# A 5x5 convolution by seven products per column instead of eight, for the first of four images

## The chip, the cores and the metric

The kernel runs on one core of a Trainium2 chip. The metric is the device time of one execution, in microseconds (us); the median of three executions is given.

## What is computed

The input x is four images of 128 channels and 64 x 64 pixels, in fp32. Four layers follow each other, each on the normalised x (a group norm over groups of four channels), each added to x:

```
x = x + attention(gn(x))            # all 4096 pixels of an image against each other
x = x + conv2d(gn(x), c, 5x5, pad 2)  # c built from two tables of weights by radius
x = x + scan(gn(x))                 # two directions, 64 channels and 64 states each
x = x + conv2d(gn(x), main_w, 3x3, pad 1) + main_b
```

The change concerns the second layer. Written for two neighbouring rows of the output, with r0 to r5 the six padded input rows under them and w0 to w4 the five rows of taps (each a row of five matrices of 128 x 128, one for each column dx), it is

```
y0 = w0 r0 + w1 r1 + w2 r2 + w3 r3 + w4 r4
y1 = w0 r1 + w1 r2 + w2 r3 + w3 r4 + w4 r5
```

which is ten products per column for a pair of rows.

## The kernel before

**The order of the images.** Channels lie on the 128 partitions, pixels along the free dimension. `program` writes the whole order out by hand, as generators: `front` makes attention, the 5x5 convolution and the operands of the scan for one image, and `scan_core` the scan. The front of image b+1 runs beside the scan of image b, piece by piece, by a budget of PE time per step. Image 0 has no scan before it, so its front runs alone: first a loop steps it until `(0, "attended")` is ready, later `before(0)` steps it until the scan's operands of image 0 are there. While image 0 is in attention, two setup generators are woven in, four steps of the front for one of theirs: `scan_constants` and `build_conv_weights`, which fills `cw` (25 matrices, and two sums of rows of taps, `SUM12` = w1 + w2 and `SUM34` = w3 + w4). In this time a pool `fill` holds side sums of the softmax (`side_sums`, on VectorE and GpSimd in turn; for the other images PE sums). The pool `tables` holds what the weights are built from.

**The convolution** is `conv_pairs`. It normalises the image in four quarters on ScalarE (`piece`, L369) into a padded image `xpe` with rows of 66 elements. GpSimd makes differences of neighbouring rows (`odd` L684, `even` L692) into `df`. The output is done in four chunks of 16 rows: eight even and eight odd ones. For each chunk three banks are accumulated, each from groups of five matmuls (L760), one for each column dx:

```
q   = (w1+w2) r2 + (w3+w4) r4
pe0 = w0 r0 + w1 (r1-r2) + w3 (r3-r4)      y0 = q + pe0
pe1 = w0 r1 + w2 (r3-r2) + w4 (r5-r4)      y1 = q + pe1
```

These are eight products for ten. A bank is taken out while the next one is filled: the closure `done` of a bank is called after the third matmul of the next. For the first image `q` is copied by ScalarE and added to both rows of `xs` by GpSimd (L775); for the others (`lean`) an identity matmul adds it on PE. `add` (L736) adds pe0 and pe1 to `xs` on VectorE with sums for the next norm, and ScalarE squares them (L313).

**After it** `scan_prep` and `scan_operands` normalise again, make the scan's operands and store them; `scan_core` loads them back (`br`, `cr`, `de`, `dx`) and GpSimd multiplies (`db`, L1027), VectorE scans (L1037), GpSimd or VectorE multiplies (L1058, L1040), PE sums over the states (L1072).

A program with a second path for softmax sums out of range follows; it isn't taken.

Of the kernel before, what the change touches and what calls it, by code (L numbers as in the profile page):

```python
# [24 lines left out]
F32 = mybir.dt.float32  # L25
I32 = mybir.dt.int32
AF = mybir.ActivationFunctionType
ALU = mybir.AluOpType
# [4 lines left out]
P = 128  # L33
# [5 lines left out]
PAD = 2  # L39
# [6 lines left out]
PRODUCT, HOP, SLOT, PACE, ENDPACE, AHEAD = 0.86, 1.7, 0.7, 2.8, 1.5, 4  # L46
# [6 lines left out]
def conv_preact_kernel(  # L53
# [16 lines left out]
    nc = tc.nc  # L70
    B, C, H, W = x.shape
# [17 lines left out]
    dram = ctx.enter_context(tc.tile_pool(name="dram", bufs=2, space=DRAM))  # L89
    ps = ctx.enter_context(tc.tile_pool(name="ps", bufs=1, space=PSUM))  # L90
    pools, ready = {}, set()

    def bank(tag, name):
        return pools.get(tag, ps).tile([P, MM], F32, tag=tag, name=name)
# [40 lines left out]
    for d in range(2):  # L135
        r = slice(d * HALF, (d + 1) * HALF)
# [81 lines left out]

    SUM12, SUM34 = 5, 6
    cw = const.tile([P, NTAP + 10, C], F32, name="cw")
    taps5 = cw[:, :NTAP, :]

# [59 lines left out]
    def large(n, name):  # L284
        return pools["big"].tile([P, ASIZE], F32, tag=f"A{n % 2}", name=name)
# [82 lines left out]
    def normalise(dst, src, gn):  # L368
        nc.scalar.activation(dst, src, AF.Identity, scale=gn[0], bias=gn[1])  # L369
# [292 lines left out]

    def conv_pairs(b, xs, tag, st, st2, lean):

        NP, CK = H // 2, CH // W // 2
        WQ = W + PAD
        xp = large(b, f"xpe_{b}")
        rows = xp[:, : HP * WQ].rearrange("p (h w) -> p h w", w=WQ)  # L670
        xh = xs.rearrange("p (h w) -> p h w", w=W)
        nc.gpsimd.memset(rows[:, :PAD, :], 0.0)
        nc.gpsimd.memset(xp[:, (HP - PAD) * WQ : HP * WQ + PAD], 0.0)
        nc.gpsimd.memset(rows[:, PAD : HP - PAD, :PAD], 0.0)
        gn = yield from group_norm(st, f"e{b}")
        diffs = pools["big"].tile([P, VSIZE], F32, tag="V", name=f"df_{b}")
        nc.gpsimd.memset(diffs[:, 2 * (NP + 1) * WQ :], 0.0)

        def piece(i):
            h0, h1 = i * H // 4, (i + 1) * H // 4  # L680
            normalise(rows[:, PAD + h0 : PAD + h1, PAD:], xh[:, h0:h1, :], gn)

        def odd(j, n):
            nc.gpsimd.tensor_tensor(  # L684
                diffs[:, j * WQ : (j + n) * WQ].rearrange("p (h w) -> p h w", w=WQ),
                rows[:, 2 * j + 1 : 2 * (j + n) : 2, :], rows[:, 2 * j + 2 : 2 * (j + n) + 1 : 2, :],
                ALU.subtract,
            )

        def even(j, n):  # L690
            at = (NP + j) * WQ
            nc.gpsimd.tensor_tensor(  # L692
                diffs[:, at : at + n * WQ].rearrange("p (h w) -> p h w", w=WQ),
                rows[:, 2 * j + 1 : 2 * (j + n) : 2, :], rows[:, 2 * j : 2 * (j + n) - 1 : 2, :],
                ALU.subtract,
            )

        def differences(i):
            last = i == 3
            odd(8 * i, 8 + last)  # L700
            even(8 * i + 1, 8 + last)

        def by_rows(t, n):

            return [t[:, o : o + n * WQ].rearrange("p (h w) -> p h w", w=WQ) for o in (0, PAD)]

        padded, differ = by_rows(xp, HP), by_rows(diffs, 2 * (NP + 1))

        def image(r, dx):
            late = dx // PAD > 0  # L710
            dx -= late * PAD
            return padded[late][:, r : r + 2 * CK - 1 : 2, dx : dx + W]

        def diff(r, dx):
            late = dx // PAD > 0
            dx -= late * PAD
            return differ[late][:, r : r + CK, dx : dx + W]

        def chunk(t, c, y):

            v = t[:, bass.ts(c, CH)].rearrange("p (h t w) -> p h t w", t=2, w=W)
            return v[:, :, y, :]

        def flat(t):
            return t.rearrange("p (h w) -> p h w", w=W)

        piece(0)
        yield HOP / 2
        piece(1)
        differences(0)  # L730
        K5 = 5
        steps, done = [], None

        def add(c, y, acc):
            i = 2 * c + y
            nc.vector.scalar_tensor_tensor(  # L736
                chunk(xs, c, y), flat(acc), 1.0, chunk(xs, c, y), ALU.mult, ALU.add,
                accum_out=st2.sum(i),
            )
            st2.squares(i, chunk(xs, c, y), xs[:, 0:1])  # L740

        for c in range(L // CH):
            j = c * CK
            if c < 2:
                piece(2 + c)
            if c < 3:
                differences(c + 1)
            accs = [
                (bank("s", f"pq_{b}_{c}"), ((SUM12, image, 2 * j + 2), (SUM34, image, 2 * j + 4))),
                (bank("a", f"pe0_{b}_{c}"),  # L750
                 ((0, image, 2 * j), (1, diff, j), (3, diff, j + 1))),
                (bank("z", f"pe1_{b}_{c}"),
                 ((0, image, 2 * j + 1), (2, diff, NP + j + 1), (4, diff, NP + j + 2))),
            ]
            for n, (acc, parts) in enumerate(accs):
                k, total = 0, len(parts) * K5
                for w, view, r in parts:
                    for dx in range(K5):
                        k += 1
                        nc.tensor.matmul(  # L760
                            flat(acc), cw[:, w * K5 + dx, :], view(r, dx),
                            start=k == 1, stop=k == total and (n == 0 or not lean),
                        )
                        if k == 3 and done is not None:
                            done()
                            done = None
                        if k % 3 == 0:
                            yield 3 * PRODUCT
                if n == 0:
                    qs = pools["bg"].tile([P, MM], F32, tag="w", bufs=4, name=f"q_{b}_{c}")  # L770

                    def done(acc=acc, qs=qs, c=c):
                        nc.scalar.copy(qs, acc)
                        for y in range(0 if lean else 2):
                            nc.gpsimd.tensor_tensor(  # L775
                                chunk(xs, c, y), chunk(xs, c, y), flat(qs), ALU.add
                            )
                    yield PRODUCT
                else:
                    if lean:  # L780
                        nc.tensor.matmul(acc, ident, qs, start=False, stop=True)
                        yield PRODUCT

                    def done(acc=acc, c=c, y=n - 1):
                        add(c, y, acc)
        yield HOP
        done()

# [351 lines left out]


    def program(safe):
        mats4, ynds, ends = {}, {}, {}
        ready.clear()
        if safe:
# [94 lines left out]
        inner, last = range(PER, NM - PER), range(NM - PER, NM)  # L1242
# [15 lines left out]
        with ExitStack() as es, tc.manual_schedule():  # L1258
# [19 lines left out]
            if not safe:  # L1278
                with tc.tile_pool(name="fill", bufs=2) as pools["fill"]:
                    while not (0, "begun") in ready:  # L1280
                        next(work)

                    with tc.tile_pool(name="tables", bufs=1) as tmp:
                        for _ in chain(scan_constants(), build_conv_weights(tmp)):
                            for _ in range(4):
                                next(work)
                    while (0, "attended") not in ready:
                        next(work)
                del pools["fill"]
                setup.close()  # L1290
# [32 lines left out]
            for _ in chain(end(B - 1, range(PER)), back(B - 1)):  # L1323
                pass

    program(False)
    lower.close()

# [12 lines left out]
    with tc.If(again > 0):  # L1341
        program(True)
# [59 lines left out]
```

## Time and profile before

| what | value |
|---|---|
| time, median of 3 | 4534.42 us (4531.9 to 4534.6) |
| span of the profiled execution | 4538.3 us |
| mean granted TensorE clock | 0.939 |
| PE busy | 4022.5 us, 89% |
| DVE busy | 3649.1 us, 80% |
| POOL busy | 3636.2 us, 80% |
| ACT busy | 2400.1 us, 53% |
| DMA | 719.48 MB, 159 GB/s on average |

The busy times are of the whole span, but the stages differ. Attention of image 0 lasts until about 507 us, its convolution from there to 653 us, and the scan's first multiplication is at 705 us. From then to about 3520 us the scan of one image runs beside the front of the next; after that the last scan runs beside the last layer of the first three images.

In the profile PE is TensorE's matmuls, PEld its loads of weights, DVE VectorE, ACT ScalarE, POOL GpSimd. A matmul of 512 columns in fp32 leaves two records.

### The profile page before, as it was taken

The page shows a single profiled execution, that of the slowest core. Times are in us where ns is not written, and L with a number is a line of the kernel's source. Part 1 is how long each engine was busy: PE and PEld are TensorE (multiplying, and loading weights), DVE is VectorE, ACT ScalarE, POOL GpSimd, SP SyncE. Part 2 cuts the span into 40 slices and gives each one's busy share as a digit, 9 for nine tenths or more (in the row PEclk, how much of TensorE's full clock was granted, in tenths as well). Part 3 has the DMA queues.
Part 4 walks back from the last instruction along what each step waited for, and adds up shares of the span by engine and source line. Part 5 has one row for each costly group of instructions (what it writes and reads, how often), then busy time and mean ns, then how long its engine had stood idle before and what let it go on. Part 6 is the DMA issues. An engine that isn't in the chain of part 4 may idle for free. (4 is left out here: it accounts for less than half of the span.)

```text
span 4538.3 us, 43660 instructions
## 1 busy us (share of the span) xinstructions
PE 4022.5 (89%) x13568; PEld 1492.3 (33%) x13568; DVE 3649.1 (80%) x3619; ACT 2400.1 (53%) x4420; POOL 3636.2 (80%) x1730
## 2 busy tenths in 40 slices
PE   8999998999999979999999879999999658576767
PEld 4444433333333323333333223333333112121212
DVE  4722106999998978999989879999999699999993
ACT  3333217666665466666654566666654654544441
POOL 3433207999998969999989889999999799999992
PEclk9999999999999989999999989999999878687878
DMA  1000006445544555544545555545445566656561
GB/s 62 6 1 1 5 29 239 175 170 174 175 174 155 181 202 201 175 174 169 179 154 181 185 207 180 169 170 175 175 159 178 211 235 204 231 188 230 186 232 47
DMA packets 210579, 719.48 MB, mean 159 GB/s; under 512 B 24864, under 2 KB 25760, under 8 KB 210208
## 3 DMA queue, kind: packets, MB, share of 16 engines
q1 hardware_dynamic: 208736, 715.87, 44.8%
q8 instruction: 109, 1.79, 0.2%
q14 instruction: 134, 1.10, 0.1%
q10 hardware_dynamic: 1600, 0.73, 0.1%
HBM read 649.07 MB, written 67.44 MB: 158 GB/s over the span
## 5 line engine op out<-in xcount | busy, mean ns | idle before, releaser
L1027 POOL TENSOR_TENSOR db<-dx,br 128x1024 f32<-128x1024 f32 x1024 | 2399.7, 2366 | 234.0 <-DMA dx<-dxd 59.7
L1020 ACT ACTIVATE da<-de,a_neg 128x512 f32<-128x512 f32 (+1 forms) x1795 | 1342.2, 751 | 745.4 <-DVE da L1037 451.2
L464 PE MATMUL sc<-r,x 128*128 128x512 f32 x2048 | 1082.4, 611 | 18.2 <-ACT r L433 12.4
L476 PE MATMUL acc<-pt,v 128*128 128x512 f32 x2048 | 1046.6, 593 | 1.6
L1058 POOL TENSOR_TENSOR hc<-hc,cr 128x1024 f32<-128x1024 f32 x406 | 959.7, 2364 | 14.3 <-ACT last L1053 11.7
L470 ACT ACTIVATE pt<-sc 128x512 f32<-128x512 f32 x1024 | 604.3, 590 | 563.9 <-PE sc L464 555.2
L1072 PE MATMUL y<-hc,sel 128*32 128x512 f32 x4096 | 656.9, 651 | 271.5 <-POOL hc L1058 267.0
L1040 DVE TENSOR_TENSOR hc<-da,cr 128x512 f32<-128x512 f32 (+1 forms) x1067 | 828.4, 776 | 68.9 <-issue 1.8
L1037 DVE TENSOR_TENSOR_SCAN da<-da,last,db 128x512 f32<-128x512 f32 (+1 forms) x464 | 728.2, 1569 | 27.3 <-POOL db L1027 21.7
L1037 DVE TENSOR_TENSOR_SCAN da<-da,da,db 128x512 f32<-128x512 f32 x449 | 577.9, 1287 | 13.6 <-ACT da L1020 12.7
L464 PEld LDWEIGHTS sc<-r,x 128*128 128x128 f32 x2048 | 359.1, 190 | 605.0 <-issue 374.3
L476 PEld LDWEIGHTS acc<-pt,v 128*128 128x128 f32 x2048 | 387.5, 190 | 497.2 <-issue 477.9
L1037 DVE TENSOR_TENSOR_SCAN hc<-da,hc,db 128x512 f32<-128x512 f32 x322 | 413.1, 1283 | 61.2 <-ACT da L1020 30.4
L1037 DVE TENSOR_TENSOR_SCAN hc<-da,last,db 128x512 f32<-128x512 f32 (+1 forms) x304 | 455.9, 1500 | 6.6 <-ACT da L1020 2.4
L518 POOL TENSOR_TENSOR sidep<-sidep,pt 128x512 f32<-128x512 f32 x120 | 170.4, 1420 | 280.0 <-ACT pt L470 277.9
L1072 PEld LDWEIGHTS y<-hc,sel 128*32 128x32 f32 x4096 | 94.7, 111 | 728.5 <-POOL hc L1058 359.5
L643 PE MATMUL pcm<-xpm,cw 128*128 128x512 f32 x576 | 290.5, 652 | 30.5 <-ACT xpm L369 30.5
L760 PE MATMUL pe<-df,cw 128*128 128x512 f32 x640 | 289.5, 598 | 0.0
L518 DVE TENSOR_TENSOR sided<-sided,pt 128x512 f32<-128x512 f32 x120 | 97.2, 810 | 231.0 <-ACT pt L470 229.7
L1037 DVE TENSOR_TENSOR_SCAN da<-da,db 128x512 f32<-128x512 f32 (+1 forms) x154 | 231.2, 1501 | 32.5 <-POOL db L1027 16.4
L498 PE MATMUL zp<-pt,ones 128*32 128x512 f32 x1536 | 204.8, 595 | 5.0 <-DVE xs L562 5.0
L1053 ACT COPY last<-da 128x1 f32<-128x1 f32 x469 | 73.0, 156 | 246.9 <-DVE hc L1040 245.1
(196 smaller groups left out, 2719.5 us busy)
## 6 DMA issues: line engine op xcount, KB each, us to landing
br<-bm SPq DMA_DIRECT2D x512, 512.0 KB, 5.2
cr<-cm SPq DMA_DIRECT2D x512, 512.0 KB, 3.9
de<-dd SPq DMA_DIRECT2D x64, 512.0 KB, 4.6
dx<-dxd SPq DMA_DIRECT2D x64, 512.0 KB, 6.5
x<-in_x_dram SPq DMA_DIRECT2D x16, 512.0 KB, 5.1
xs<-in_x_dram SPq DMA_DIRECT2D x16, 512.0 KB, 5.6
xsd<-xs SPq DMA_DIRECT2D x16, 512.0 KB, 5.1
xcd<-xc SPq DMA_DIRECT2D x16, 512.0 KB, 2.8
```

Of the source, the lines that this page charges most:

```text
L464: nc.tensor.matmul(sc, xn[:, bass.ts(j, P)], rq[blk], start=True, stop=True)
L470: nc.scalar.activation(pt, sc, AF.Exp)
L476: nc.tensor.matmul(acc[blk], v[:, j, :], ring[:, u % NRING, :], start=j == 0, stop=j == NJT - 1)
L518: eng.tensor_tensor(s, s, ring[:, u % NRING, :], ALU.add)
L643: nc.tensor.matmul(acc.rearrange("p (r w) -> p r w", w=W), weights[:, t, :], xp[:, y : y + RPM, dx : dx + W], start=t == 0, stop=t == k * ...
L760: nc.tensor.matmul(flat(acc), cw[:, w * K5 + dx, :], view(r, dx), start=k == 1, stop=k == total and (n == 0 or not lean),)
L1020: nc.scalar.activation(da, rep["de", b, c, d, g][:, bass.ts(h, size)], AF.Exp, scale=a_neg[:, at(i)])
L1027: nc.gpsimd.tensor_tensor(dbs[i], rep["dx", b, c, d, g], rows["b", b, c, d, q], ALU.mult)
L1037: nc.vector.tensor_tensor_scan(h, da, db[:, cut], before, ALU.mult, ALU.add)
L1040: nc.vector.tensor_tensor(hc[:, cut], h, rows["c", b, c, d, q][:, cut], ALU.mult)
L1058: nc.gpsimd.tensor_tensor(hcs[i], hcs[i], rows["c", b, c, d, q], ALU.mult)
L1072: nc.tensor.matmul(y[r : r + SG, :], sel, hcs[i - KG + 1 + gg][:, bass.ts(h, MM)], start=q == 0, stop=False, tile_position=(0, r), skip_gr ...
```

## The change

For the first image the three upper rows of taps are done in another way. With three sums of rows, t = r1 + r2, f = r0 - r2 and l = r3 - r1, and two more rows of matrices, HSUM = (w0 + w1 + w2) / 2 and HDIF = (w0 - w1 + w2) / 2:

```
q   = (w3+w4) r4 + HSUM t
pm  = HDIF (r1-r2)
pe0 = w0 f + w3 (r3-r4)                    y0 = q - pm + pe0
pe1 = w2 l + w4 (r5-r4)                    y1 = q + pm + pe1
```

These are seven products for ten. The sums of rows are made by VectorE (`combine`, three instructions for each quarter, into `combos`), the matrices by VectorE too (`more_weights`, four instructions, woven in behind `build_conv_weights`). pm has a bank of its own (tag `y`) and is taken out by VectorE, subtracted from the even rows and added to the odd ones. `combos` and `more` lie in the pool `fill`, which therefore stays open until the convolution is done. The other three images are left as they were.

The diff, cut to its core:

```diff
+    def more_weights(to):
+        w = [cw[:, n * 5 : (n + 1) * 5, :] for n in range(3)]
+        half, dif = to[:, 0], to[:, 1]
+        nc.vector.tensor_tensor(half, w[0], w[2], ALU.add)
+        yield HOP
+        nc.vector.tensor_scalar(half, half, 0.5, None, ALU.mult)
+        yield HOP
+        nc.vector.scalar_tensor_tensor(dif, w[1], -0.5, half, ALU.mult, ALU.add)
+        yield HOP
+        nc.vector.scalar_tensor_tensor(half, w[1], 0.5, half, ALU.mult, ALU.add)
+        yield HOP
...
+        wide = pools.get("fill") if not lean else None
+        if wide:
+            NC = NP * WQ + PAD
+            combos = wide.tile([P, 3, NC], F32, tag="combos", bufs=1, name="combos")
+            nc.gpsimd.memset(combos[:, :, NP * WQ :], 0.0)
+            views = [by_rows(combos[:, n, :], NP) for n in range(3)]
+
+        def combine(j, n):
+            for m, (p, q, op) in enumerate(
+                ((1, 2, ALU.add), (0, 2, ALU.subtract), (3, 1, ALU.subtract))
+            ):
+                a, b_ = (rows[:, 2 * j + r : 2 * (j + n) + r - 1 : 2, :] for r in (p, q))
+                nc.vector.tensor_tensor(views[m][0][:, j : j + n, :], a, b_, op)
+
         def differences(i):
             last = i == 3
+            if wide:
+                combine(8 * i, 8)
             odd(8 * i, 8 + last)
             even(8 * i + 1, 8 + last)
...
+            if wide:
+                total, first, last = (combo(n) for n in range(3))
+                accs = [
+                    (accs[0][0], (accs[0][1][1], (HSUM, total, j))),
+                    (bank("y", f"pm_{b}_{c}"), ((HDIF, diff, j),)),
+                    (accs[1][0], ((0, first, j), (3, diff, j + 1))),
+                    (accs[2][0], ((2, last, j), (4, diff, NP + j + 2))),
+                ]
...
+                elif wide and n == 1:
+                    def done(acc=acc, c=c):
+                        for y, op in enumerate((ALU.subtract, ALU.add)):
+                            nc.vector.tensor_tensor(
+                                chunk(xs, c, y), chunk(xs, c, y), flat(acc), op
+                            )
...
+                    more = pools["fill"].tile([P, 2, 5, C], F32, tag="more", bufs=1, name="more")
 
                     with tc.tile_pool(name="tables", bufs=1) as tmp:
-                        for _ in chain(scan_constants(), build_conv_weights(tmp)):
+                        for _ in chain(scan_constants(), build_conv_weights(tmp), more_weights(more)):
                             for _ in range(4):
                                 next(work)
-                    while (0, "attended") not in ready:
+                    while (0, "convolved") not in ready:
                         next(work)
                 del pools["fill"]
                 setup.close()
```

More of the change, by code (lines that the diff above doesn't have):

```diff
@@ L91, in conv_preact_kernel @@
     pools, ready = {}, set()
+    more = None
     def bank(tag, name):
@@ L217, in scan_constants @@
         yield HOP
-    SUM12, SUM34 = 5, 6
+    SUM12, SUM34, HSUM, HDIF = 5, 6, 7, 8
     cw = const.tile([P, NTAP + 10, C], F32, name="cw")
@@ L677, in conv_pairs, with by_rows @@
         nc.gpsimd.memset(diffs[:, 2 * (NP + 1) * WQ :], 0.0)
+        def by_rows(t, n):
+            return [t[:, o : o + n * WQ].rearrange("p (h w) -> p h w", w=WQ) for o in (0, PAD)]
         def piece(i):
@@ L696, in even @@
             )
+        wide = pools.get("fill") if not lean else None
[10 more added lines that the diff above has]
+                nc.vector.tensor_tensor(views[m][0][:, j : j + n, :], a, b_, op)
         def differences(i):
             last = i == 3
+            if wide:
+                combine(8 * i, 8)
             odd(8 * i, 8 + last)
             even(8 * i + 1, 8 + last)
-        def by_rows(t, n):
-            return [t[:, o : o + n * WQ].rearrange("p (h w) -> p h w", w=WQ) for o in (0, PAD)]
         padded, differ = by_rows(xp, HP), by_rows(diffs, 2 * (NP + 1))
@@ L717, in diff, with combo, view @@
             return differ[late][:, r : r + CK, dx : dx + W]
+        def combo(n):
+            def view(r, dx):
+                late = dx // PAD > 0
+                dx -= late * PAD
+                return views[n][late][:, r : r + CK, dx : dx + W]
+            return view
         def chunk(t, c, y):
@@ L760, in conv_pairs @@
                         nc.tensor.matmul(
-                            flat(acc), cw[:, w * K5 + dx, :], view(r, dx),
-                            start=k == 1, stop=k == total and (n == 0 or not lean),
+                            flat(acc), cw[:, w * K5 + dx, :] if w < HSUM else more[:, w - HSUM, dx, :],
+                            view(r, dx), start=k == 1, stop=k == total and (n == 0 or not lean),
                         )
@@ L782, in conv_pairs, with done @@
                         yield PRODUCT
-                    def done(acc=acc, c=c, y=n - 1):
+                    def done(acc=acc, c=c, y=n - len(accs) + 2):
                         add(c, y, acc)
@@ L787, in conv_pairs @@
         done()
+        ready.add((b, "convolved"))
     def scan_prep(b, xs, st, mats4):
@@ L1144, in program @@
     def program(safe):
+        nonlocal more
         mats4, ynds, ends = {}, {}, {}
```

## The prediction

> **What bounds the kernel now.** I read the page first (busy shares, slices), then the table of busy time by stretch, then the first image's convolution in the waits and the timeline.
>
> From the page, the slices (113 us each; columns are tenths busy):
>
> ```profile
> span 4538.3 us, 43660 instructions
> PE   8999998999999979999999879999999658576767
> DVE  4722106999998978999989879999999699999993
> POOL 3433207999998969999989889999999799999992
> ```
>
> In slices 2 to 5 only PE is full. From slice 6 on, VectorE and GpSimd (the scan) are full as well. The changed convolution lies in slices 4 and 5, where nothing runs beside it. The stretches (columns: us, then busy PE, PEld, DVE, ACT, POOL, granted clock, DMA share, GB/s):
>
> ```profile
> 513.30:653.40 140.10, 140.02 (x320) 61.01 (x320) 4.89 (x14) 11.61 (x22) 18.80 (x16) 0.99 0.01 4
> 653.40:697.00 43.60, 33.76 (x118) 11.57 (x120) 12.03 (x28) 27.69 (x43) 5.73 (x7) 0.92 0.45 168
> 780.00:1500.00 720.00, 702.87 (x2626) 259.40 (x2630) 673.96 (x706) 441.17 (x886) 666.89 (x296) 0.99 0.49 170
> ```
>
> The convolution takes 140.1 us and PE is busy in 140.0 of them; DVE works 4.9 us and POOL 18.8. What PE waits for between 514 and 652 us is a single line, the wait that ends as the stage begins:
>
> ```profile
> PE pq L760 <- ACT xpe L369: 7.6, 1, 7.6
> ```
>
> So the stage is bound by the number of matmuls. The timeline gives their price and the stage's two ends (start, duration, what, and in brackets the idle time before it):
>
> ```profile
> 512.01 3.51 ACT L369 ACTIVATE xpe<-xs,nb_e,rs_e 128x1024 f32<-128x1024 f32 x3 [3.91 <-POOL df L677]
> 513.30 10.78 PE L760 MATMUL pq<-xpe,cw 128*128 128x512 f32 x20 [7.65 <-ACT xpe L369]
> ...
> 523.92 4.49 PE L760 MATMUL pe<-xpe,cw 128*128 128x512 f32 x10
> 528.24 8.75 PE L760 MATMUL pe<-df,cw 128*128 128x512 f32 x20
> ...
> 558.39 1.89 PE L760 MATMUL pe<-xpe,cw 128*128 128x512 f32 x4
> ...
> 653.43 0.69 DVE L736 SCALAR_TENSOR_TENSOR xs<-pe,xs 128x512 f32<-128x512 f32 x1 [12.22 <-PE pe L760]
> ```
>
> A matmul leaves two records: 320 records, 4 chunks of 40 matmuls. From 523.92 to 558.39 runs exactly one chunk: 34.47 us / 40 = 0.862 us each. The first ten took 10.62 us instead of 8.62: about 2.0 us go to the slow clock at the start. PE starts at 513.30, as the first of three normalising pieces ends; at the far end VectorE's last addition is released by PE at 653.43.
>
> Behind it everything hangs on that end. GpSimd's queue:
>
> ```profile
> 689.46 2.49 POOL L889 TENSOR_TENSOR delta<-delta,u 128x512 f32<-128x512 f32 x2 [30.55 <-ACT u L913]
> ...
> 705.14 2.35 POOL L1027 TENSOR_TENSOR db<-dx,br 128x1024 f32<-128x1024 f32 x1 [10.75 <-DMA br<-bm]
> ```
>
> GpSimd waits 30.55 us for this image's operands, and the scan's first product waits for a transfer of rows just written by this image. No clock, other image or earlier load sets the start of the scan.
>
> [...] PE idles 7.65 us, then loses about 2.0 us in its first ten matmuls. The idle gap only grows, so this loss stays. [...] The trace has 692 ns (the scan's multiply, L1040, 780 to 3500 us) and 1825 ns for 1600 elements. [...] between 100 and 230 us, where both sum, the side sums take 1053 ns on DVE and 1760 on POOL, against 0.69 and 1.27 us apart.
>
> **The change, part by part.**
>
> *Removed and replaced on PE.* Each chunk had 8 groups of five matmuls (2 in pq, 3 in each pe); now 7 (2 in pq, 1 in pm, 2 in each pe). Four chunks: 160 becomes 140. Same shape, both operands fp32, views of the same stride for diffs and combos (rows back to back, as diffs had). 20 x 0.862 = 17.2 us off a stage in which PE never waits.
>
> *The start.* Before, the first five matmuls read the rows of the first normalised quarter alone; now the first group is SUM34, whose rows begin two lower and reach into the second quarter. The three pieces take 3.51 us together, 1.17 each: PE starts at about 514.47 instead of 513.30. Cost 1.2 us, on the path.
>
> *Three sums of rows, 12 on VectorE.* 12 x 0.71 = 8.5 us, in a stage where DVE works 4.9 of 140. PE waits for them at two kinds of place. First chunk: the fourth matmul of the second group reads two elements over the edge and so needs the fourth sum. Six sums and four differences are queued on DVE and POOL from 513.3 on; [...] they take 6 x 0.71 + 4 x 1.12 (POOL L684, L692) = 8.7 us and end at 522.0. PE asks at 514.47 + 2.0 + 8 x 0.862 = 523.4. Hidden, by a margin of 1.4 us. Later chunks: the sums wait for the normalised piece, which ACT does behind the squares of pe0; from pe0's end that is 0.3 + 0.8 (DVE) + 1.1 + 1.2 (ACT) + 0.7 = 4.1 us, and PE has 18 matmuls, 15.5 us, before it asks. Hidden behind pe1. What queues behind a waiting sum on DVE is the addition of pe1, which no one needs within a chunk.
>
> *pm's eviction, 8 on VectorE.* One PSUM and one SBUF input, nearest row L561, 0.69 us: 5.5 us. Each pair waits for POOL's additions of q (2 x 1.27), released about 0.8 us after pq ends; pm's own five matmuls take 4.3. A bank of its own (y), unused until the scan. Hidden.
>
> *The two matrices.* Four instructions of 640 elements during attention. Bounds: [...] 1.29 by the nearest row, L274 (beside POOL); together 3.3 to 5.2 us. I take the high end. There DVE lags behind the side sums by up to 5.7 us (a sum ready at 182.0 runs at 187.7), with the added one 7.0. The ring has 8 places of 1.72 us, 13.7 us, so ScalarE doesn't wait for a place and PE doesn't either. Cost 0.
>
> *Moved.* The early pools close after the convolution instead of after attention. The scan's tiles keep their places and their first loads come later anyway. On every engine the order outside these instructions is unchanged. Cost 0.
>
> *Sum.* -17.2 + 1.2 = -16.0 us; the last addition at about 637.4 instead of 653.43, and all behind it earlier by the same. 4534.4 - 16.0 = 4518.4 us.
>
> **The rivals.**
>
> R1, part of the gain is lost on the spot. For: the margin of 1.4 us at the first chunk, DVE's lag in the build of the weights[...]. Against: PE's single wait in the stage. Two of the three together cost about 2 to 6 us: 4520 to 4524, say 4523.
>
> R2, the gain doesn't reach the end. The scan stage (POOL 93% busy from 780 to 1500 us) would have to start when it did before, because another wait takes over: 4534. For: PE, DVE and POOL are all near full later, so a different phase of transfers could cost some us. Against: the 30.55 us wait above; nothing on POOL or DVE between 653 and 689 us comes from elsewhere.
>
> R3, slower: PE waits for the new sums in every chunk. If each chunk began with its three sums, two differences and two additions in series (2.1 + 2.2 + 2.5 = 6.9 us) and PE stood still meanwhile, 27.6 us would be lost: 4518.4 + 27.6 = 4546. Against: the operations are issued a chunk ahead, as the differences are now, and PE waits for none of those.
>
> R4, more than the count: later stages fall into a better phase, 4510. Nothing speaks for it.
>
> **How the numbers follow.** Forecast 0.77, R1 0.13, R2 0.05, R3 0.03, R4 0.02. The predicted time is the forecast's, 4518.4. The range takes in R1 and the scatter of the three times (4531.9 to 4534.6) with some us for phases of the scan on both sides: 4512 to 4525.5. Within 0.2% means over 4525.4. Faster: forecast, R1, R4, 0.92; same: R2, 0.05; slower: R3, 0.03.
>
> **What would show it.** Right: 280 records of matmuls in the stage, beginning about 514.5 and ending near 637; no PE wait in it; four groups of DVE sums near 0.7 us; a first db near 689. Start wrong: PE begins at 513.3. R1: a wait of PE for combos, or for pt in attention. R2: POOL's first db still near 705. R3: four waits on DVE inside the stage. The forecast fails if the first db moves by 16 us and the end doesn't.

## The result, and the profile after

The changed kernel takes 4521.68 us (median of 10 executions, 4515.17 to 4524.64), the kernel before 4534.45 us beside it (10 executions, 4529.49 to 4536.89). The ratio is 0.9971, with a 95% interval of 0.9963 to 0.998: 12.8 us shorter, between 9.1 and 16.8. The forecast was 4518.4 us, with a range of 4512 to 4525.5.

The page of the changed kernel, the lines for its span and the busy slices (113 us each):

```profile
span 4517.3 us, 43608 instructions
...
PE   8999998999999979999999879999999658575767
DVE  4721217999998978999989879999999799999992
POOL 3433308999998969999989789999999899999992
```

The slices are counted from 0. VectorE's slices 4 and 5 went from 1 and 0 tenths to 2 and 1: that is the new work, in a stage where it was nearly idle. In slice 6 VectorE went from 6 to 7 and GpSimd from 7 to 8: the scan begins earlier in that slice.

Busy time by stretch of the changed kernel (us, then busy PE, PEld, DVE, ACT, POOL, clock, DMA share, GB/s):

```profile
513.00:636.50 123.50, 121.94 (x280) 53.30 (x280) 21.51 (x35) 11.63 (x22) 20.87 (x18) 0.98 0.01 5
636.50:681.00 44.50, 34.97 (x122) 11.79 (x122) 12.39 (x29) 28.18 (x43) 5.59 (x5) 0.92 0.47 171
```

280 records instead of 320: 20 matmuls fewer. PE is busy for 121.94 us, where it was 140.02. VectorE works 21.51 us instead of 4.89. What PE waits for between 512 and 636 us is still one line:

```profile
PE pq L808 <- ACT xpe L370: 8.9, 1, 8.9
```

No sum, no eviction and no difference holds PE up. The wait in front of the first matmul grew from 7.6 to 8.9 us. The timeline shows the two ends and the first chunk (start, duration, what, in brackets the idle time before it), first what feeds PE, then PE, then the way to the scan:

```profile
511.74 3.51 ACT L370 ACTIVATE xpe<-xs,nb_e,rs_e 128x1024 f32<-128x1024 f32 x3 [3.90 <-POOL nb_e L365]
...
513.01 7.48 DVE L731 TENSOR_TENSOR combos<-xpe 128x528 f32<-128x528 f32 x6 [2.21 <-ACT xpe L370]
...
513.06 1.62 POOL L705 TENSOR_TENSOR df<-xpe 128x528 f32<-128x528 f32 x1 [1.28 <-ACT xpe L370]
...
514.25 5.95 PE L808 MATMUL pq<-xpe,cw 128*128 128x512 f32 x10 [8.87 <-ACT xpe L370]
520.04 4.46 PE L808 MATMUL pq<-combos,more 128*128 128x512 f32 x10
524.33 4.46 PE L808 MATMUL pm<-df,more 128*128 128x512 f32 x10
528.62 4.46 PE L808 MATMUL pe<-combos,cw 128*128 128x512 f32 x10
...
545.79 4.49 PE L808 MATMUL pq<-xpe,cw 128*128 128x512 f32 x10
...
575.87 4.49 PE L808 MATMUL pq<-xpe,cw 128*128 128x512 f32 x10
...
636.23 0.69 DVE L776 SCALAR_TENSOR_TENSOR xs<-pe,xs 128x512 f32<-128x512 f32 x1 [7.89 <-PE pe L808]
...
672.30 2.49 POOL L944 TENSOR_TENSOR delta<-delta,u 128x512 f32<-128x512 f32 x2 [30.59 <-ACT u L968]
...
687.28 2.37 POOL L1082 TENSOR_TENSOR db<-dx,br 128x1024 f32<-128x1024 f32 x1 [10.07 <-DMA br<-bm]
```

PE starts 514.25 - 511.74 = 2.51 us behind the first normalising instruction; before it was 513.30 - 512.01 = 1.29. The groups that read sums or differences take 4.29 us for five matmuls. One chunk, from 545.79 to 575.87, takes 30.08 us where it took 34.47. The stage, from its first normalising instruction to its last addition, is 124.49 us long where it was 141.42: 16.9 us less. The scan's first db comes 17.9 us earlier than in the profile of before (705.14). Both are one pair of profiles; further ones follow below.

### The profile page after: what moved, and what is told of

It reads as the page before. It is cut to its first block, busy times and chain, and to the rows that moved or that the text cites. A ratio compares the mean times of both kernels' runs of the same rounds, so it can differ in the third digit from the quotient of the medians.

```text
span 4517.3 us, 43608 instructions
## 1 busy us (share of the span) xinstructions
PE 3996.2 (88%) x13528; PEld 1482.2 (33%) x13528; DVE 3667.9 (81%) x3643; ACT 2399.5 (53%) x4420; POOL 3638.5 (81%) x1731
## 5 line engine op out<-in xcount | busy, mean ns | idle before, releaser
L1113 POOL TENSOR_TENSOR hc<-hc,cr 128x1024 f32<-128x1024 f32 x406 | 960.1, 2365 | 17.6 <-ACT last L1108 15.1
L1092 DVE TENSOR_TENSOR_SCAN da<-da,last,db 128x512 f32<-128x512 f32 (+1 forms) x464 | 728.1, 1569 | 24.1 <-POOL db L1082 17.6
L1092 DVE TENSOR_TENSOR_SCAN da<-da,da,db 128x512 f32<-128x512 f32 x449 | 577.9, 1287 | 14.3 <-ACT da L1075 13.4
L808 PE MATMUL pe<-df,cw 128*128 128x512 f32 x560 | 255.2, 598 | 0.0
```

The lines of the kernel that those rows point to most:

```text
L808: nc.tensor.matmul(flat(acc), cw[:, w * K5 + dx, :] if w < HSUM else more[:, w - HSUM, dx, :], view(r, dx), start=k == 1, stop=k == total ...
L1092: nc.vector.tensor_tensor_scan(h, da, db[:, cut], before, ALU.mult, ALU.add)
L1113: nc.gpsimd.tensor_tensor(hcs[i], hcs[i], rows["c", b, c, d, q], ALU.mult)
```

## The experiments

All times are compared with executions of the kernel before on the same chip. A difference in us is that of the two medians. The ratio with its interval weighs all executions, so it needn't be the ratio of the medians; where only five executions were made the two can lie 2 to 4 us apart. The kernels with matmuls left out no longer compute the convolution; they only price the matmuls. "Matmuls" are those of the first image's convolution unless others are named.

**The changed kernel again, and matmuls left out of the kernel before.** The time had fallen by 12.8 us, the stage in the profile by 16.9. Either a part is lost behind the stage, or the additions cost something, or single executions scatter too much for the difference to mean anything. The first four kernels ask this.

The changed kernel, unaltered:

> The changed kernel unaltered, as the yardstick for the runs on the same chip. Theory S (every us taken off the first convolution reaches the end, the missing 3 us of the first comparison are scatter between executions): 16 to 18 us faster than the kernel before. Theory L (a fixed few us, or a quarter, are lost in the later stages): 12 to 13.5 us faster again.

Measured: 4518.57 us against 4532.9; 14.3 us shorter, ratio 0.9969 (0.9958 to 0.998). It lies between the two theories and doesn't choose. Its profile shows one source of scatter. The first two groups of PE:

```profile
516.09 7.53 PE L808 MATMUL pq<-xpe,cw 128*128 128x512 f32 x10 [8.87 <-ACT xpe L370]
523.46 4.46 PE L808 MATMUL pq<-combos,more 128*128 128x512 f32 x10
```

The first five matmuls took 7.37 us here and 5.79 in the profile above, behind the same idle time of 8.87 us; five at a granted clock of 1.00 take 4.29. The slow start costs 3.1 us in one execution and 1.5 in the other.

Twenty matmuls left out of the kernel before:

```diff
+            if not lean:
+                accs[2] = (accs[2][0], accs[2][1][:2])
```

> The kernel before without its last group of five matmuls in pe1 of the first image (w4 times r5-r4 is left out of the odd rows): 20 matmuls fewer, none of the new sums, no later start. Theory S: first db 17.2 us earlier and the time 17.2 us shorter. Theory L: db 17.2 us earlier and the time 13 us shorter. Theory V (what the change adds on VectorE or the pool held longer costs the 3 us): 17.2 us here, and only some 13 in the changed kernel on the same chip.

Measured: 4512.48 us against 4532.9; 20.4 us shorter, ratio 0.9959 (0.9945 to 0.9972), which is 18.6 us (12.7 to 24.9). Its first db is at 689.13 us, 176 us behind the first normalising instruction where it was 193. No loss shows on the way to the end; theory L's 13 us lies at the interval's edge.

Forty left out:

```diff
+            if not lean:
+                accs[1:] = [(t, parts[:2]) for t, parts in accs[1:]]
```

> As the run with 20 matmuls fewer, and the last group of pe0 left out too (w3 times r3-r4 of the even rows, w4 times r5-r4 of the odd ones): 40 matmuls fewer. Theory S: 34.5 us shorter. Theory L with a fixed loss of 4 us: 30.5. Theory L with a quarter lost: 26.

Measured: 4497.07 us; 35.8 us shorter, ratio 0.9929 (0.9916 to 0.9943), which is 32 us (25.8 to 38.1). The medians say theory S, the ratio lies between theory S and a fixed loss of 4 us. A loss of a quarter stands at the very edge of the interval; a fixed loss can't be excluded by this run alone.

Sixty left out of the other three images, where the scan runs beside the convolution:

```diff
+            if lean:
+                accs[2] = (accs[2][0], accs[2][1][:2])
```

> The kernel before with the last group of pe1 left out for the other three images (w4 times r5-r4 of their odd rows), 60 matmuls fewer where the scan runs beside them. If PE sets the pace there as in the first image: 51.7 us shorter. If GpSimd and VectorE set it: within 5 us of the kernel before. I expect the second, 0 to 10 us shorter.

Measured: 4528.81 us against 4532.9; 4.1 us shorter, ratio 0.9994 (0.9986 to 1.0003). 51.7 us of PE's work are gone and about a tenth of it shows at most (6.3 us at the interval's edge). The stretch from 1500 to 2500 us of this kernel:

```profile
1500.00:2500.00 1000.00, 949.20 (x3450) 350.53 (x3448) 918.23 (x980) 602.12 (x1157) 907.22 (x410) 0.98 0.52 181
```

PE is 95% busy there, as in the kernel before, yet its matmuls aren't what is paid for. VectorE and GpSimd are at 92 and 91%; that they set the pace there agrees with this, but isn't shown by it. The first image is the place for this change, since there a matmul taken away shows in the time.

**The start and the clock.** Two kernels price the two terms at the stage's beginning, a third has both edits. The quarters of normalising cut one row later:

```diff
             h0, h1 = i * H // 4, (i + 1) * H // 4
+            if not lean:
+                h0, h1 = h0 + (i > 0), min(h1 + 1, H)
```

> The changed kernel with the first image's quarters of normalising cut one row later (17, 16, 16 and 15 rows), so that the first group of matmuls needs only the first piece. If the later start costs what I priced: PE begins 1.3 us after the first normalising instruction instead of 2.5, and the time is 1.1 us shorter than the changed kernel's (some 15 us shorter than the kernel before), which the trace shows and the times hardly can. If the first group waits for something else as well: no change in PE's beginning.

Measured: 4518.26 us against 4532.9; 14.6 us shorter, ratio 0.9967 (0.9955 to 0.9979). ScalarE and PE at the start:

```profile
510.89 3.56 ACT L370 ACTIVATE xpe<-xs,nb_e,rs_e 128x1088 f32<-128x1088 f32 x3 [3.90 <-POOL nb_e L365]
...
512.24 6.21 PE L810 MATMUL pq<-xpe,cw 128*128 128x512 f32 x10 [7.70 <-ACT xpe L370]
```

PE follows after 1.35 us instead of 2.51. The later start was the wait for the second piece and nothing else. In the time it doesn't stand out, as expected.

Eight matmuls without use in PE's idle time:

```diff
+        if not lean:
+            idle = bank("y", f"idle_{b}")
+            for _ in range(8):
+                nc.tensor.matmul(
+                    idle, ident, cw[:, :4, :].rearrange("p k c -> p (k c)"), start=True, stop=True
+                )
         gn = yield from group_norm(st, f"e{b}")
```

> The changed kernel with eight matmuls of 512 columns, whose result nothing reads, put into PE's idle time in front of the first convolution. If the slow clock after that idle time costs 1.5 to 3 us and differs from execution to execution: the ten matmuls of the first bank take 8.6 us instead of 10 to 12, and the time is 1.5 to 3 us shorter than the changed kernel's. If the clock is no part of the missing time: the same as the changed kernel.

Measured: 4520.56 us; 12.3 us shorter, ratio 0.9972 (0.9961 to 0.9983): no gain over the changed kernel. The timeline and the clock (third number from the end of each line in the second fence, PE's busy time behind the comma) say why:

```profile
505.31 7.03 PE L695 MATMUL idle<-cw,ident 128*128 128x512 f32 x16
514.34 6.25 PE L814 MATMUL pq<-xpe,cw 128*128 128x512 f32 x10 [2.00 <-ACT xpe L370]
520.42 4.46 PE L814 MATMUL pq<-combos,more 128*128 128x512 f32 x10
```

```profile
510.96:514.37 3.41, 1.42 (x5) 0.38 (x3) 1.28 (x2) 2.55 (x3) 2.05 (x5) 1.00 0.00 0
514.37:517.78 3.41, 3.41 (x4) 1.42 (x5) 3.41 (x3) 0.95 (x1) 3.41 (x3) 0.50 0.00 0
517.79:519.79 2.00, 2.00 (x6) 0.94 (x5) 2.00 (x2) 0.00 (x0) 1.59 (x2) 1.00 0.00 0
```

The eight ended 2.00 us too soon. Just as the convolution began, at 514.37, the clock went to half, and the first five matmuls took 6.08 us. The expectation failed: the filling left 2.00 us of idle time in front of the stage, and the start stayed slow.

Both edits:

> Both edits together: the stage from the first normalising instruction to the last addition takes 1.3 + 140 x 0.86 + 0.4 = 122 us instead of 124.5 to 126; 2.6 to 4 us shorter than the changed kernel, 17 to 19 us shorter than the kernel before.

Measured: 4514.07 us against 4532.9; 18.8 us shorter, ratio 0.9956 (0.9943 to 0.997). PE and the clock again:

```profile
506.01 7.03 PE L695 MATMUL idle<-cw,ident 128*128 128x512 f32 x16
513.88 4.59 PE L816 MATMUL pq<-xpe,cw 128*128 128x512 f32 x10 [0.83 <-ACT xpe L370]
518.31 4.46 PE L816 MATMUL pq<-combos,more 128*128 128x512 f32 x10
```

```profile
513.00:515.00 2.00, 1.17 (x4) 0.65 (x4) 1.14 (x2) 2.00 (x3) 1.09 (x1) 1.00 0.00 0
515.00:517.00 2.00, 2.00 (x6) 0.79 (x5) 2.00 (x2) 1.10 (x1) 2.00 (x2) 1.00 0.00 0
```

With the earlier start the gap is 0.83 us, the clock stays at 1.00, and the first five matmuls take 4.43 us. The last addition of the stage comes 121.97 us after its first normalising instruction, as expected, and 2.5 us sooner than in the changed kernel's profile. By its median this is the fastest kernel that leaves nothing out, but its interval overlaps with the changed kernel's.

**What the additions cost.** Each sum of rows issued twice:

```diff
-                nc.vector.tensor_tensor(views[m][0][:, j : j + n, :], a, b_, op)
+                for _ in range(2):
+                    nc.vector.tensor_tensor(views[m][0][:, j : j + n, :], a, b_, op)
```

> The changed kernel with each of the twelve sums of rows issued twice: 8.5 us more on VectorE. If the sums are hidden, as priced: the time of the changed kernel, within its scatter, except at the first chunk, where twelve sums and four differences in series end at about 526 us and PE asks for the fourth sum at 523.4: up to 3 us there. If the sums cost the missing 3 us: another 3 us or more in every chunk's waits, and a time 3 to 8 us longer.

Measured: 4518.32 us, 14.6 us shorter than before, ratio 0.9968 (0.9956 to 0.9979): what the changed kernel gives. The sums of the first two quarters and all of PE's waits in the stage:

```profile
513.79 11.68 DVE L732 TENSOR_TENSOR combos<-xpe 128x528 f32<-128x528 f32 x12 [2.21 <-ACT xpe L370]
```

```profile
PE pq L809 <- ACT xpe L370: 8.9, 1, 8.9
```

Twice the sums still hide, at the first chunk too. The twelve end at 525.47, as expected, but PE needs only the first four: the fourth is written for the second time by 522.75, and PE asks for it at 523.7. The 3 us allowed for the first chunk didn't come.

After these eight the kernels with the new products came out some 2 us short of what their stage gains, and those with matmuls left out did not. The last four ask about that. The changed kernel with its additions, but the old eight groups on PE, in two runs:

```diff
-            if wide:
+            if False:
                 total, first, last = (combo(n) for n in range(3))
...
-                elif wide and n == 1:
+                elif False:
```

> The changed kernel with all its additions but the old eight groups of matmuls: the sums of rows and the two matrices are made on VectorE and the pool is held, nothing reads them. So far the kernels with the new products come out some 2 us short of what their stage gains, the two with matmuls left out do not (both with intervals of 2 to 3 us). Theory V, the additions cost it: 2 to 3 us slower than the kernel before. Theory S, scatter: the same as the kernel before within 1.5 us.

> The same kernel once more, for more executions: the same expectations.

Measured: 4533.9 and 4533.71 us against 4533.32, 13 executions of this kernel each; both ratios 1.0001 (0.9992 to 1.0009). The medians are 0.6 and 0.4 us longer, and the intervals exclude a cost of more than some 4 us for the sums, the matrices and the pool held longer. Theory V's 2 to 3 us lie inside these intervals; the 26 executions taken together average 0.2 us more than the 26 of the kernel before, which speaks against it. pm's eviction is not in this kernel. The changed kernel's profile has it, here in the last chunk:

```profile
619.13 1.28 DVE L830 TENSOR_TENSOR xs<-xs,pm 128x512 f32<-128x512 f32 x2 [12.28 <-PE pm L808]
...
627.64 0.69 DVE L776 SCALAR_TENSOR_TENSOR xs<-pe,xs 128x512 f32<-128x512 f32 x1 [7.23 <-PE pe L808]
```

VectorE has taken pm out 7.23 us before PE releases the next addition, so this eviction holds nothing up in the stage.

> The changed kernel once more, beside the one with 20 matmuls left out on the same chip. Theory S: 1 to 2 us slower than that one (its later start of 1.2 us), 16 us faster than before. Theory V or L: 3 to 5 us slower than that one, 13 to 14 us faster than before.

> The kernel with 20 matmuls left out (w4 times r5-r4 of the first image's odd rows) once more: 17.2 us faster than before by theory S, 13 to 14 by theory L.

Measured: the changed kernel 4517.99 us, 15.3 us shorter, ratio 0.9967 (0.9955 to 0.9979); with 20 matmuls left out 4514.41 us, 18.9 us shorter, ratio 0.9963 (0.9949 to 0.9977). The medians differ by 3.6 us, within the 3 to 5 of theories V and L; the ratios lie 1.8 us apart, within the 1 to 2 of theory S. With 6 and 5 executions that is no choice.

**Where the executions scatter.** The time from the first db to the end of the span, from each profile (span minus start of db):

| kernel | first db, us | span, us | from db to the end, us |
|---|---|---|---|
| before | 705.14 | 4538.3 | 3833.2 |
| additions only, two runs | 706.37, 705.72 | 4529.3, 4531.6 | 3822.9, 3825.9 |
| 20 matmuls left out, two runs | 689.13, 687.39 | 4514.7, 4510.0 | 3825.6, 3822.6 |
| 40 matmuls left out | 672.06 | 4490.6 | 3818.5 |
| changed, three runs | 687.28, 691.93, 687.91 | 4517.3, 4519.1, 4514.3 | 3830.0, 3827.2, 3826.4 |
| changed, each sum twice | 689.07 | 4513.9 | 3824.8 |
| changed, start cut; PE filled; both | 686.37, 688.16, 687.26 | 4515.7, 4517.8, 4517.7 | 3829.3, 3829.6, 3830.4 |

Within one kernel the rest of the program varies by several us between profiles. The value of the kernel before stands apart: its profile is of an execution of 4540.09 us, longer than any of the 69 timed executions of this kernel (4526.5 to 4537.8). With it, the six profiles with the old products average 3824.8 us from the first db to the end, without it 3823.1. The seven with the new products average 3828.3. So the profiles don't show that all of the stage's gain reaches the end. They rather speak for 3 to 5 us more behind the first db in the kernels with the new products, but single differences of this size are no more than the scatter.

## Why the prediction was right

**The price of a matmul.** Forecast 20 x 0.862 = 17.2 us. PE's waits inside the stage are none, and four chunks, each 34.47 - 30.08 = 4.39 us shorter, give 17.6 us. The 0.4 us more come from the mix: five matmuls take 4.29 us in the groups that read sums or differences and 4.32 or 4.33 in those that read the padded image (523.92 to 528.24 before, 545.79 to 550.12 after), and six of the seven groups are now of the first kind, four of the eight before. Shown, by the profile and by the kernels with 20 and 40 matmuls left out.

**The later start.** Forecast 1.2 us; the profile has 2.51 - 1.29 = 1.22, and cutting the quarters one row later takes it back. Shown.

**The slow clock.** I took its 2.0 us for a constant, an estimate from one trace. The start of the changed kernel lost 1.5 and 3.1 us in two executions. The stretches at half rate, in the kernel before, the changed kernel and its repeat:

```profile
506.89:517.12 10.23, 3.81 (x5) 1.75 (x6) 2.89 (x15) 4.32 (x5) 4.57 (x7) 0.50 0.00 0
506.84:517.07 10.23, 2.81 (x4) 1.29 (x5) 6.72 (x19) 4.32 (x5) 4.83 (x7) 0.50 0.00 0
505.07:522.12 17.05, 8.08 (x15) 4.30 (x16) 11.25 (x22) 4.32 (x5) 7.06 (x8) 0.50 0.00 0
```

Half rate ended 3.8, 2.8 and 6.0 us after PE's first matmul (513.30, 514.25 and 516.09), and half of that is about what each lost. In the traces of the kernel before and the changed kernel the granted clock is either 1.00 or 0.50, and every stretch between two changes is a multiple of 3.413 us; the stretches above are three, three and five times that long. The moment of the change shifts against PE's work: half rate began 1.2 and 1.5 us after PE's idle time had begun in the first two, and 2.2 us before it in the repeat. For the mean the constant is fair (five profiles with the new products and no filling lose 2.0 us on average), for a single execution it isn't. With it the stage's gain in the first pair of profiles comes out: 17.6 - 1.2 + 0.5 = 16.9 us.

**The sums.** Forecast hidden, by 1.4 us at the first chunk, with the six sums and four differences one after the other, which was an estimate. Its 0.71 us for a sum lies on the line through two lengths that the kernel before shows (692 ns for 512 elements, 1825 ns for 1600), which gives 709 ns for 528. Six sums at the 0.70 us of the later ones would take 4.2 us; they took 7.48, the slowest of them 1.63, and a difference 1.62 us where it was 1.10. They ended at 520.49. PE asked at 520.04 + 3 x 0.86 = 522.6: a margin of 2.1 us. The two engines do slow each other here, but less than by whole instructions one after the other, which would be the 8.7 us of the forecast. The later sums took 0.70 us each, as forecast. Issued twice the sums are hidden still.

**pm's eviction.** Forecast 8 x 0.69 us on VectorE, hidden. The median of the eight is 0.684 us, and VectorE is done with it 7 us before its next work. Shown, by the profile.

**The matrices.** Forecast 3.3 to 5.2 us on VectorE, hidden; the lower bound was an estimate, 0.82 us for each of the four (the same line gives 825 ns for 640 elements). The tile's instructions in the changed kernel (min/median/max in ns, and the start):

```profile
L673 DVE TENSOR_TENSOR more<-cw x1: 1883/1883/1883, 187.4 to 187.4; 128x640 f32<-128x640 f32 x1
L675 DVE TENSOR_SCALAR more<-more x1: 1558/1558/1558, 190.6 to 190.6; 128x640 f32<-128x640 f32 x1
L677 DVE SCALAR_TENSOR_TENSOR more<-cw,more x1: 819/819/819, 193.5 to 193.5; 128x640 f32<-128x640 f32 x1
L679 DVE SCALAR_TENSOR_TENSOR more<-cw,more x1: 820/820/820, 199.5 to 199.5; 128x640 f32<-128x640 f32 x1
```

Together 5.1 us; two of the four are stretched to twice the others. The convolution's first normalising instruction is at 511.74 instead of 512.01. In all the profiles it lies between 510.9 and 513.6, and the changed kernel's three (511.7 to 513.6) are among those of the kernels with the old products (511.7 to 513.3), so no loss in attention shows.

**The way to the end.** Forecast: all behind the stage is earlier by the same, 16.0 us. Stage and first db did that: between the kernels with the old products and nothing left out and the changed kernel, in the mean of three profiles each, the stage is 16.6 us shorter and the first db 16.7 us earlier. The times say 12.8, 14.3 and 15.3 us in three comparisons. 16.0 lies within each interval, but each median falls short of it. The means of the same executions differ by 13.1, 14.1 and 15.1 us, 14.1 on average; by the scatter of the executions I estimate that this is good to some 1.3 us. So about 2 us of what the stage gains probably don't reach the end. The forecast put this at nothing, with the words "all behind it earlier by the same", and its range took the difference in. What the loss is stays open. The sums, the matrices and the pool show no such cost by themselves, pm's eviction holds nothing up, and the kernels with 20 matmuls left out, whose stage is as short, gave 18.6 and 16.8 us by their ratios, with no loss to be seen.

Of the rivals, R2 (the scan starts when it did before) and R3 (waits in every chunk) are ruled out by the first db and by PE's single wait. R1's idea that some of it goes on the spot is right for the clock alone, whose loss was 3.1 us in one profile instead of the 2.0 of before. Of R4's gain beyond the count nothing is seen.

## What to carry to other kernels

Where one image runs alone and PE never waits, matmuls left out paid in full as far as the scatter lets one see. Replacing 20 of them was worth 13 to 15 us net here, while 60 in stages where PE is 95% busy beside a scan were worth 4. Look at who else is busy in that stretch, not at PE's share. When a product is replaced, look at what its first reader now needs: a group that reaches one row into the next piece cost 1.2 us at the start, and cutting the pieces one row later gave it back.

## What was not expected of the hardware

Idle time of 2.00 us in front of the convolution was followed by a fall of TensorE's clock to half, although it had been 1.00 until then, from the eight matmuls on; with 0.83 us it stayed at 1.00. Each is one profile, and no rule follows from the two. In the trace half rate lasted from 514.37 to 517.78, 3.41 us, with PE busy throughout. In the 3.41 us before it PE was busy for 1.42 us. Filling idle time only in part left the loss as it was: the first five matmuls took 6.08 us against 5.79 with no filling, and 4.43 when the filling reached up to 0.83 us before.
